# Running the masked weight's first products ahead of the layer norm, on raw x

## The chip, the cores and the metric

The kernel runs on one core of a Trainium2 chip (trn2). The time is the device time of one execution in microseconds (us), taken as the median of several runs. The core has a matrix engine (TensorE, "PE" in the profile; its weight loads are "PEld"), three engines for elementwise work (VectorE "DVE", ScalarE "ACT", GpSimd "POOL") and SyncE ("SP"), which issues the DMAs here. Each engine takes its instructions in the order in which the program lists them.

## The reference

```python
x  = data                                  # (2, 1024, 512), float32
xn = layernorm(x)                          # per token, eps 1e-5, no weight
w_masked = weight * (32x32 block of mask has a non-zero sum)    # (512, 512)
s  = einsum('bsk,nk->bsn', xn, w_masked)
nx = rmsnorm(xn) * ln_w
h  = silu(nx @ gate_w.T) * (nx @ up_w.T)   # 1792 features
g  = silu(h @ down_w.T)
out = x + s * g
```

All is float32. The 2048 tokens are four token tiles of 512 columns, and the 512 features are four chunks of 128 rows.

## The kernel before

All matrix products are done by a two-level Strassen-like scheme (the Winograd variant) on blocks. The outer level splits rows of the weight, features and tokens in two and has seven products per weight group, `q` = 1 to 7; each of them is again seven products of a 128x128 weight with a 128x512 operand, `m` = 1 to 7. One `(g, q)` is an *instance* of seven products (`instance`); a product is two matmul instructions in the profile.

There are eight weight groups. Groups 0 to 6 are pieces of the gate and up weights; group 7, called `G`, is the masked weight. The program runs `q` = 1 and 2 of all groups first (phase 1: 16 instances, group after group), then `q` = 6, 5, 7, 3, 4 of all groups (phase 2), then the product with the down weight (`down_instance`). For `q` = 1 and 2 only token tiles 0 and 1 are needed.

Nothing is scheduled by the compiler: each step is entered with `at(pos, fn)`, the events are sorted by `pos`, and each engine gets its instructions in that order. One position is the time of one product on TensorE. Instance `j` puts its products at `7*j` plus 0, 2, 3, 4, 6, 8 and 12 (for `m` = 1, 5, 2, 6, 3, 7, 4) unless the table `EARLY` says otherwise. `T(us)` turns a planned time at the start into a position.

The start: x tiles 0 and 1 are loaded by token rows, `stats` takes mean and variance on VectorE, `factors` makes scale and shift (ScalarE square root, VectorE reciprocal), `normalise` applies them, TensorE transposes the tiles (`transpose`), and `evacuate` copies them out of PSUM. TensorE meanwhile multiplies an identity (`warm`). Token tiles 2 and 3 are treated otherwise: they are loaded already transposed (`load_xt`), and their scale and shift, which then lie along the columns, are turned into rows on TensorE (`fac_rows`), stored to DRAM, read back as a broadcast over the partitions (`fac_bc`) and applied on GpSimd (`scale_xt`).

PSUM banks are taken by tag: X has 3, Y 2, Z 1 and V 2 (`PSB`). A V bank is used for anything short-lived: transposed tiles, `fac_rows`, mask sums, gates.

GpSimd also makes the sums of weight blocks (`inner_a`, four ops per instance pair, around seven positions ahead of it), some of the operand differences (`inner_b`, `outer_b`) and the masking (`mask_a`). Group `G` comes last in phase 1, so its mask is loaded at position 15, summed at 46 to 53 (`mask_rows`), gathered over 32x32 blocks by a small matmul (`mask_blocks`) at 79.5, and applied around position 90. The sums that group `g` keeps for phase 2 lie in `acc` (four tiles) and are stored to `acc_dram[g]`; the finished part of `s` goes to `s_dram`.

Of the kernel before, what the change touches and what calls it, by code (L numbers as in the profile page):

```python
# [14 lines left out]
P = 128  # L15
# [16 lines left out]
def tile_masked_linear_gated_ffn(  # L32
# [22 lines left out]
    fac_dram = tc.dram_tile([2, 2, W], F32, name="fac_dram")  # L55
# [11 lines left out]
    EARLY = {}  # L67
# [42 lines left out]
    def constants():  # L110
        nc.gpsimd.memset(eps2, EPS * EPS)
        make_identity(nc, ident)
        nc.scalar.activation(stat_0, eps2, AF.Sqrt)
        nc.gpsimd.memset(blockones, 0.0)
        for b in range(P // BLK):
            nc.gpsimd.memset(blockones[b * BLK : (b + 1) * BLK, b * BLK : (b + 1) * BLK], 1.0)
# [4 lines left out]
    fac = small.tile([P, 2, 2, TT], F32, tag="fac", name="fac", bufs=1)  # L121
    rms = small.tile([P, NTT, TT], F32, tag="rms", name="rms", bufs=1)

    def load_x(t):
        for i in range(TT):
            xt[t, i] = mem[:, first_slot[("B6", "vc", "v5", "B4")[t]] + i, :]
            nc.sync.dma_start(xt[t, i], x[(t * TT + i) * P : (t * TT + i + 1) * P, :])
# [6 lines left out]
    def factors(t, i=0, n=TT):  # L134


        if t < 2:
            scl = small.tile([P, n], F32, tag="scl", name=f"scl_{t}_{i}", bufs=3)
            nb = small.tile([P, n], F32, tag="nb", name=f"nb_{t}_{i}", bufs=3)
        else:  # L140
            scl, nb = fac[:, t - 2, 0, :], fac[:, t - 2, 1, :]
# [69 lines left out]
    def fac_rows(t):  # L211
        b = bank("V", f"fac_rows_{t}")
        nc.tensor.transpose(b[: 2 * TT, :P], fac[:, t - 2].rearrange("p f i -> p (f i)"), ident)
        rows = small.tile([2 * TT, P], F32, tag="rows", name=f"fac_sb_{t}")
        nc.scalar.copy(rows, b[: 2 * TT, :P])
        nc.sync.dma_start(fac_dram[t - 2].rearrange("f (i p) -> (f i) p", p=P), rows)
        for f in range(2):
            fac_bc[t, f] = mem[:, F["B6"] + 3 + 2 * (t - 2) + f, :]
            nc.sync.dma_start(fac_bc[t, f], fac_dram[t - 2, f].unsqueeze(0).to_broadcast([P, W]))
# [62 lines left out]
    def operand(q, m):  # L282
# [17 lines left out]

    def load_a(g, K):
        aq[g, 0, K] = mem[:, F["a1"] + 2 * (g % 3) + K, :]
        nc.sync.dma_start(aq[g, 0, K], gu[g, 0, K] if g < G else wm[0, K])
# [50 lines left out]
    def mask_blocks():  # L354
        pm = bank("V", "pm")
        nc.tensor.matmul(pm[:, :64], blockones, mask_sums.rearrange("p a b -> p (a b)"), start=True, stop=True)
        nc.vector.tensor_scalar(keep.rearrange("p a b -> p (a b)"), pm[:, :64], 0.0, None, ALU.is_gt)

    def mask_a(v, R, K):
        v = v.rearrange("p (b j) -> p b j", j=BLK)  # L360
        k = keep[:, 2 * R + K, :].unsqueeze(2).to_broadcast([P, 16, BLK])
        nc.gpsimd.tensor_tensor(v, v, k, ALU.mult)

    def inner_a(g, part, k0=0, n=2):

        if part == 1:
            i, si, qs = F["a1"] + 2 * (g % 3), F["s"] + 2 * (g % 2), (1, 2)
# [17 lines left out]
    def instance(j, g, q, prior, dest, after):  # L385
# [4 lines left out]
        seeded = j > 1  # L390

        def mm(m, tag, key, first):
            if first and key not in st:
                st[key] = bank("Y" if key == "z" and j == 1 else tag, f"{key}_{j}")
            nc.tensor.matmul(st[key], weights(g, q, m), operand(q, m), start=first and not (key == "z" and seeded),  # L395
                             stop=True, skip_group_check=True)

        def seed():
# [4 lines left out]
            else:  # L403
                st["s1"] = slot("s2" if j else "s5", f"s1_{j}")
# [23 lines left out]
        for off, m, tag, first, snapshot, out in (  # L428
# [8 lines left out]
            key, pos = tag.lower(), 7 * j + off  # L437
# [3 lines left out]
            elif out:  # L441

                pos += 2.3 if prior is None and m == 2 and seeded else 1
# [6 lines left out]
    def group(g, where):  # L450
# [3 lines left out]
        acc, v5, c1 = tiles(F["acc"] + 4 * (g % 2)), tiles(F["v5"] + 4 * (g % 2)), tiles(F["c1"] if g % 2 else F["vc"])  # L454
# [17 lines left out]
        def done(R, Hh, tiles):  # L472
# [3 lines left out]
            def after(i, pos):  # L476
                r, n = divmod(i, 2)
                if g == G:
                    at(pos + 1, lambda: nc.sync.dma_start(s_dram[2 * R + r, 2 * Hh + n], tiles(i)))
# [10 lines left out]
        def summed(dst, src, into, then=None, engines=(pool,) * 4):  # L490
# [9 lines left out]
            1: (None, acc, nothing),  # L500
            2: (acc, c1, done(0, 0, c1)),
# [16 lines left out]
        at(7 * where[g, 1] + 15, lambda: nc.sync.dma_start(acc_dram[g], sums))  # L518
# [117 lines left out]
    def down_instance(o, q, where_, prior, dest, after):  # L636
# [78 lines left out]
        if last_set:  # L715
            at(where_(17) + 0.1, base_of_last)
            for part, pos in zip(parts, (where_(23), where_(24), where_(25))):
# [6 lines left out]
    order = [(g, q) for g in range(G + 1) for q in (1, 2)]  # L724
# [4 lines left out]
    T = lambda us: (us - 14.0) / 0.86  # L729
    EARLY.update({(0, 1): T(10.4), (0, 2): T(11.3), (1, 1): T(12.1), (1, 2): T(13.0), (0, 0): T(11.5), (1, 0): 4.3,  # L730
                  (0, "z"): 2.2, (1, "z"): 4.5})
    SILU = 26.2
    at(T(-10), constants)
    at(T(-10), load_x, 0)
    at(T(-10), lambda: nc.scalar.dma_start(lnw_sb, ln_w))

    at(T(-10), lambda: nc.gpsimd.tensor_copy(mem[:, F["a1"], 0:1], xt[0, 0][:, 0:1]))
    at(T(-10), load_a, 0, 0)
    at(T(-10), load_x, 1)
    at(T(-10), load_a, 0, 1)  # L740

    at(T(9.95), lambda: nc.gpsimd.memset(mem[:, F["a1"] + 2, 0:1], 0.0))
    for K in range(2):
        at(T(9.96), load_a, 1, K)
    at(T(9.96), load_x, 2)
    for K in range(2):
        at(T(9.96), load_a, 2, K)
    at(T(9.96), load_x, 3)
# [8 lines left out]

    at(T(1.4), lambda: warm(22, bank("V", "idle")))
    plan(T(4.9), 0, factors(0, 0, 2))
    plan(T(7.1), 0, factors(0, 2, 2))  # L760
    for t, p, step in ((1, T(12.5), 0), (3, 23.2, 0.6), (2, 36.1, 1.2)):
        plan(p, step, factors(t))
    for us, i, h in ((5.9, 0, 0), (6.0, 0, 1), (6.1, 1, 0), (7.2, 1, 1), (7.95, 2, 0), (8.4, 2, 1), (7.95, 3, 0), (8.4, 3, 1)):
# [223 lines left out]
```

## Time and profile before

| | |
|---|---|
| median of 3 runs | 507.12 us (506.67 to 507.19) |
| profiled execution: span from the first to the last instruction | 504.8 us |
| PE / DVE / ACT / POOL busy | 99% / 74% / 37% / 71% of the span |
| matmul 128x512, mean of one | 593 ns (two to a product; they are pipelined) |
| POOL 128x512 tensor op | 1322 ns mean |
| DVE 128x512 tensor op | 686 ns mean |
| ACT 128x512 copy | 573 to 597 ns mean |
| DMA | 124.75 MB, 247 GB/s mean over the span |

The profile is of one execution, whose span is 504.8 us; the runs' times have a median 2.3 us above that. A line of a timeline gives the start, the duration, engine, source line, operation, the tiles written and read, the count, and in square brackets how long the engine had been idle before and what ended that. `L98` is the helper `add`, through which all tensor-tensor ops go. "Waits" and "idle" are inferred from semaphore events.

### The profile page before, as it was taken

What the parts mean: (1) busy time and instruction counts of PE and PEld (TensorE: products, weight loads), DVE (VectorE), ACT (ScalarE), POOL (GpSimd) and SP (SyncE); (2) the same over time, 40 slices, a digit from 0 to 9 for tenths busy, and PEclk for the clock granted to TensorE, in tenths of its full rate; (3) what the DMA queues carried; (4) which work ended last, traced back from release to release, by engine and by line L of the source; (5) the groups of instructions that cost most, each with busy time, mean ns of one, the idle gap of its engine ahead of it and who ended that gap; (6) DMA issues with size and microseconds to landing.
All of it is one profiled execution on the core that took longest, in us unless ns stands there. A gap on an engine that the chain in (4) does not pass through costs nothing.

```text
span 504.8 us, 4923 instructions
## 1 busy us (share of the span) xinstructions
PE 499.2 (99%) x1231; PEld 227.4 (45%) x1231; DVE 375.6 (74%) x578; ACT 188.1 (37%) x362; POOL 358.8 (71%) x301
## 2 busy tenths in 40 slices
PE   8999999999999999999999999999999999999996
PEld 7444444444444444444444444444444444444444
DVE  6887887876968969697896969879657644377636
ACT  6667775734535363443535333330101101001111
POOL 5629997464886959879696999985672764649960
PEclk9999999999999999999999999999999999999999
DMA  6878746368178594876949475599996798467362
GB/s 208 306 234 335 292 168 250 123 251 293 62 245 295 186 329 181 295 240 244 335 154 317 179 265 213 216 351 387 365 335 221 253 389 311 130 238 269 106 229 84
DMA packets 62221, 124.75 MB, mean 247 GB/s; under 512 B 5968, under 2 KB 13552, under 8 KB 60144
## 3 DMA queue, kind: packets, MB, share of 16 engines
q1 hardware_dynamic: 62048, 124.43, 69.1%
q8 instruction: 10, 0.16, 0.1%
q14 instruction: 19, 0.16, 0.1%
q10 hardware_dynamic: 144, 0.00, 0.0%
HBM read 78.25 MB, written 46.15 MB: 246 GB/s over the span
## 4 chain that ended last, share of the span: by engine, by line
PE 97%; DVE 1%; ACT 1%; DMA 1%; issue 0%; DVEq 0%; ACTq 0%
PE x L395 38%; PE y L395 19%; PE dx L643 15%; PE z L395 10%; PE dy L643 8%; PE dz L643 5%; PE dv L643 1%; PE pt L165 1%; DMA mem<-in_x 1%; DVE mem L98 0%; ACT mem L158 0%; DVE st L131 0%; DVE mem L633 0%; ACT silu L626 0%; ACT scl L150 0%
## 5 line engine op out<-in xcount | busy, mean ns | idle before, releaser
L98 POOL TENSOR_TENSOR mem<-mem 128x512 f32<-128x512 f32 (+4 forms) x261 | 322.1, 1257 | 111.6 <-ACT mem L423 30.5
L395 PE MATMUL x<-mem 128*128 128x512 f32 x448 | 211.7, 593 | 0.0
L395 PEld LDWEIGHTS x<-mem 128*128 128x128 f32 x448 | 84.6, 190 | 107.3 <-issue 89.7
L98 DVE TENSOR_TENSOR mem<-x,mem 128x512 f32<-128x512 f32 x137 | 93.4, 686 | 42.1 <-PE x L395 40.4
L395 PE MATMUL y<-mem 128*128 128x512 f32 x224 | 114.6, 593 | 0.1
L643 PE MATMUL dx<-mem 128*128 128x512 f32 x174 | 78.3, 592 | 0.0
L98 DVE TENSOR_TENSOR mem<-mem 128x1536 f32<-128x1536 f32 (+3 forms) x50 | 66.9, 1342 | 6.9 <-PE dx L643 4.4
L98 DVE TENSOR_TENSOR mem<-y,mem 128x512 f32<-128x512 f32 x96 | 65.9, 686 | 7.9 <-PE y L395 6.5
L402 ACT COPY z<-x 128x512 f32<-128x512 f32 x54 | 30.9, 573 | 94.7 <-PE x L395 91.7
L395 PEld LDWEIGHTS y<-mem 128*128 128x128 f32 x224 | 42.2, 190 | 53.1 <-issue 46.5
L395 PE MATMUL z<-mem 128*128 128x512 f32 x112 | 57.3, 593 | 0.0
L643 PEld LDWEIGHTS dx<-mem 128*128 128x128 f32 x174 | 33.1, 190 | 41.6 <-issue 40.9
L643 PE MATMUL dy<-mem 128*128 128x512 f32 x98 | 44.5, 592 | 0.0
L461 ACT ACTIVATE gate<-mem 128x512 f32<-128x512 f32 x56 | 32.7, 602 | 20.4 <-DVE mem L98 15.9
L466 DVE TENSOR_TENSOR mem<-gate,mem 128x512 f32<-128x512 f32 x56 | 38.1, 682 | 1.9 <-ACT gate L461 1.5
L616 POOL TENSOR_TENSOR mem<-mem 128x512 f32<-128x512 f32 x16 | 25.8, 1619 | 13.6 <-DMA mem<-s_dram 13.4
L626 ACT ACTIVATE silu<-mem 128x512 f32<-128x512 f32 x15 | 9.0, 602 | 64.6 <-DVE mem L98 48.3
L395 PEld LDWEIGHTS z<-mem 128*128 128x128 f32 x112 | 21.1, 190 | 25.9 <-issue 21.4
L98 DVE TENSOR_TENSOR mem<-z,mem 128x512 f32<-128x512 f32 x41 | 28.1, 685 | 2.8 <-PE z L395 2.7
L643 PEld LDWEIGHTS dy<-mem 128*128 128x128 f32 x98 | 18.6, 190 | 23.4 <-issue 23.2
L98 DVE TENSOR_TENSOR mem<-dx,mem 128x512 f32<-128x512 f32 x16 | 11.1, 691 | 20.3 <-PE dx L643 20.2
L643 PE MATMUL dz<-mem 128*128 128x512 f32 x56 | 25.2, 592 | 0.0
(86 smaller groups left out, 286.9 us busy)
## 6 DMA issues: line engine op xcount, KB each, us to landing
h_dram<-mem SPq DMA_DIRECT2D x98, 256.0 KB, 2.2
mem<-h_dram SPq DMA_DIRECT2D x28, 768.0 KB, 6.7
mem<-in_gu SPq DMA_DIRECT2D x42, 256.0 KB, 3.9
acc_dram<-mem SPq DMA_DIRECT2D x8, 1024.0 KB, 4.0
mem<-acc_dram SPq DMA_DIRECT2D x8, 1024.0 KB, 6.1
mem<-in_x_t SPq DMA_DIRECT2D x24, 256.0 KB, 5.5
mem<-in_x SPq DMA_DIRECT2D x16, 256.0 KB, 4.5
s_dram<-mem SPq DMA_DIRECT2D x16, 256.0 KB, 6.1
```

The costliest lines, as they stand in the source:

```text
L98: eng.tensor_tensor(o, a, b, op)
L165: nc.tensor.transpose(pt[t, c][:, i * P : (i + 1) * P], xt[t, i][:, c * P : (c + 1) * P], ident)
L395: nc.tensor.matmul(st[key], weights(g, q, m), operand(q, m), start=first and not (key == "z" and seeded), stop=True, skip_group_check=True)
L402: nc.scalar.copy(st["z"], st["x"])
L461: nc.scalar.activation(gate[key], t(), AF.Silu)
L466: nc.vector.tensor_mul(a(), gate[key], b())
L616: at_later.append(lambda: nc.gpsimd.tensor_tensor(s_tile, s_tile, rms_bc[t], ALU.mult))
L626: nc.scalar.activation(b[0][:, part], y[:, part] if source is None else source(), AF.Silu)
L643: nc.tensor.matmul(st[key], w(), b(), start=first and key != "z", stop=True, skip_group_check=True)
```

## The change

Group `G` now comes first in phase 1 (`order`), as instances 0 and 1. Its operands are token tiles 0 and 1 of x itself, loaded transposed and not normalised (`load_raw`, `raw_b`). Since the layer norm of a token is `scl * x + nb`, its product with a weight row is `scl` times the raw product plus `nb` times the sum of that row. The row sums are taken on TensorE with a column of ones (`row_sum`, `row_sums`), and the eight finished tiles (four kept sums, four of `s`) are multiplied by the broadcast `scl` on GpSimd, the outer product of `nb` and the row sums is made on ScalarE, and GpSimd adds it (`amend`, steps 0, 1, 2). For this, tiles 0 and 1 get broadcast factors through `fac_rows` as tiles 2 and 3 have.

Group 0 and all that goes with it move 14 positions later (`S`); the plan's times at the start have a new origin (`R_`); the work between positions 62 and 104 is moved by less and less (`late`), and phase 2 stays where it was. The mask's first two quarters are loaded first of all; the loads of the start are issued in one row without the two small ops that held some of them back. The warm-up is 9 and 2 products instead of 22.

```diff
+        nc.gpsimd.memset(ones, 1.0)
-    fac = small.tile([P, 2, 2, TT], F32, tag="fac", name="fac", bufs=1)
+    fac = small.tile([P, NTT, 2, TT], F32, tag="fac", name="fac", bufs=1)
...
     def fac_rows(t):
         b = bank("V", f"fac_rows_{t}")
-        nc.tensor.transpose(b[: 2 * TT, :P], fac[:, t - 2].rearrange("p f i -> p (f i)"), ident)
+        nc.tensor.transpose(b[: 2 * TT, :P], fac[:, t].rearrange("p f i -> p (f i)"), ident)
...
+    def load_raw(c, t):
+        xr[c, t] = mem[:, F["B7" if c > 1 else "B5"] + 2 * t + c % 2, :]
+        nc.sync.dma_start(xr[c, t], x_t[c, t])
+
+    def raw_b(q, m, eng):
+        b11, b12, b21, b22 = (xr[2 * (q - 1) + k, n] for k in (0, 1) for n in (0, 1))
+        o = mem[:, F["B3"] + 2 + q if m == 4 else F[("B5", "B7")[q - 1]] + m - 1, :]
+        a, b = {5: lambda: (b12, b11), 6: lambda: (b22, rop[q, 5]), 7: lambda: (b22, b12),
+                4: lambda: (b21, rop[q, 6])}[m]()
+        add(eng, o, a, b, ALU.subtract)
+        rop[q, m] = o
...
+    def row_sum(K, r, k):
+        if not rs:
+            rs[0] = bank("V", "rsums")
+        c = 2 * K + r
+        nc.tensor.matmul(rs[0][:, c : c + 1], aq[G, 0, K][:, (2 * k + r) * P :][:, :P], ones, start=k == 0, stop=k == 1,
+                         skip_group_check=True)
+
+    def row_sums():
+        nc.scalar.copy(rsum[:, 0:2], rs[0][:, 0:2])
+        nc.vector.tensor_add(rsum[:, 2:4], rs[0][:, 2:4], rsum[:, 0:2])
+
+    def amend(i, src, o, part, of, step):
+        r, n = divmod(i, 2)
+        if step == 0:
+            add(pool, o, src, fac_bc[n, 0], ALU.mult)
+        elif step == 1:
+            nc.scalar.mul(part, fac_bc[n, 1], rsum[:, of + r : of + r + 1])
+        else:
+            add(pool, o, o, part)
...
+            kept, s11 = F["B5"], F["B7"]
+            for n, i in enumerate((0, 1, 3, 2)):
+                for step, pos in enumerate((AMEND[0], AMEND[1] - 1.5, AMEND[1])):
+                    at(pos + 1.5 * n, lambda i=i, n=n, step=step: amend(i, acc1(i), mem[:, kept + i, :],
+                                                                        mem[:, kept + 4 + n % 3, :], 0, step))
+                    at(pos + 6 + 1.5 * n, lambda i=i, n=n, step=step: amend(i, c1(i), mem[:, s11 + i, :],
+                                                                            mem[:, s11 + 4 + n % 3, :], 2, step))
+                at(AMEND[1] + 7 + 1.5 * n, lambda i=i: nc.sync.dma_start(s_dram[i // 2, i % 2], mem[:, s11 + i, :]))
+            at(AMEND[1] + 6, lambda: nc.sync.dma_start(acc_dram[G], slots(kept, 4)))
...
-    order = [(g, q) for g in range(G + 1) for q in (1, 2)]
+    order = [(g, q) for g in (G, *range(G)) for q in (1, 2)]
...
+    R_ = lambda us: (us - 8.7) / 0.86
+    S = 14
+    late = lambda p: p + S if p < 62 else p + S * (104 - p) / 42 if p < 104 else p
+    RAW.update({jm: R_(5.05 + 0.86 * k) for k, jm in enumerate(
+        ((0, 1), (0, 2), (0, 5), (0, 6), (0, 3), (0, 7), (1, 1), (0, 4), (1, 2), (1, 5), (1, 6), (1, 3), (1, 7)))})
+    RAW[1, 4] = R_(17.0)
+    AMEND = (22.0, 34.0)
...
-    at(T(1.4), lambda: warm(22, bank("V", "idle")))
+    at(R_(1.4), lambda: warm(9, bank("V", "idle")))
+    at(R_(4.4), lambda: warm(2, bank("V", "idle2")))
+    for K, p in ((0, 3.5), (1, 7.65)):
+        at(R_(p), mask_rows, 0, K)
+        at(R_((4.2, 8.45)[K]), mask_blocks, K, 1)
+        at(R_((4.5, 8.9)[K]), mask_keep)
+    for us, b0, b1, eng in ((4.55, 0, 4, dve), (4.6, 8, 12, dve), (4.65, 4, 8, pool), (4.7, 12, 16, pool)):
+        at(R_(us), lambda b0=b0, b1=b1, eng=eng: mask_a(aq[G, 0, 0], 0, 0, eng, b0, b1))
+    at(R_(8.95), lambda: mask_a(aq[G, 0, 1], 0, 1, dve))
+    for us, q, m, eng in ((6.0, 1, 5, dve), (6.6, 1, 6, dve), (7.3, 1, 7, pool), (8.6, 1, 4, pool),
+                          (12.0, 2, 5, dve), (13.2, 2, 6, dve), (13.3, 2, 7, pool), (14.5, 2, 4, pool)):
+        at(R_(us), raw_b, q, m, eng)
...
-    for t, p, step in ((1, T(12.5), 0), (3, 23.2, 0.6), (2, 36.1, 1.2)):
+    for t, p, step in ((1, R_(19.2), 0), (3, S + 23.2, 0.6), (2, S + 36.1, 1.2)):
         plan(p, step, factors(t))
...
+    at(S + 5.5, fac_rows, 0)
+    at(S + 5.9, fac_rows, 1)
...
-    at(25.2, fac_rows, 3)
+    at(S + 25.2, fac_rows, 3)
```

## The prediction

> **What bounds it now.** I read the page's span, busy lines and chain that ended last, then timelines: the first 22 us, GpSimd's, and all engines and SyncE around 31 to 36 us.
>
> ```profile
> span 504.8 us, 4923 instructions
> PE 97%; DVE 1%; ACT 1%; DMA 1%; issue 0%; DVEq 0%; ACTq 0%
> ```
>
> TensorE (PE) is the chain from 8.8 us on. The end moves only if PE starts useful work earlier, does more, or stops. The start, from the timeline (start, duration, engine, line, op):
>
> ```profile
> 1.37 6.97 PE L756 MATMUL idle<-ident 128*128 128x128 f32 x44 [1.37 <-POOL ident masks.py:199]
> 3.50 0.69 DVE L131 BATCH_NORM_STATS2 st<-mem 128x6 f32<-128x512 f32 x1 [3.50 <-DMA mem<-in_x]
> 13.11 1.38 DVE L156 TENSOR_SCALAR mem<-mem,scl,nb 128x256 f32<-128x256 f32 x4
> 15.69 1.13 PE L395 MATMUL y<-mem 128*128 128x512 f32 x2
> 17.11 0.14 PEld L165 LDWEIGHTS pt<-ident,mem 128*128 128x128 f32 x1 [0.26 <-ACT mem L173]
> 19.69 0.68 DVE L98 TENSOR_TENSOR mem<-pt,mem 128x512 f32<-128x512 f32 x1
> ```
>
> Until 8.2 us PE only warms up. VectorE (DVE) normalises x from 3.50 to 14.49. From 15.69 (group 0's product m=5, position 2) PE is dense: a product (two matmuls) each 0.86 us. So the prize is a few us. At 17.11 PE waits for a PSUM bank of tag V until ScalarE (ACT) has read it: there are two V banks.
>
> GpSimd's timeline:
>
> ```profile
> 20.45 4.26 POOL L98 TENSOR_TENSOR mem<-mem 128x512 f32<-128x512 f32 x5 [0.69 <-DVE mem L98]
> 29.94 3.02 POOL L98 TENSOR_TENSOR mem<-mem 128x256 f32<-128x256 f32 x4 [5.23 <-ACT mem L316]
> 39.10 15.08 POOL L98 TENSOR_TENSOR mem<-mem 128x512 f32<-128x512 f32 x14 [6.13 <-DMA mem<-fac_dram]
> ```
>
> The first row is `inner_b` (2,4), 1.24 us, and `inner_a` of group 1 (four of about 0.7); the second is `inner_a` of group 2; then it waits for the broadcast factors and is full. The factors' route, from the timelines of all engines and of SyncE (SP):
>
> ```profile
> 31.27 0.30 ACT L150 ACTIVATE fac<-agg,eps 128x4 f32<-128x4 f32 x1
> ...
> 33.74 0.27 PE L213 MATMUL fac_rows<-ident,fac 128*8 128x128 f32 x1
> ...
> 34.33 0.34 SPq L216 DMA_DIRECT2D fac_dram<-fac_sb  x1
> 35.69 0.90 SPq L219 DMA_DIRECT2D mem<-fac_dram  x2
> ```
>
> ACT's copy of the rows starts at 34.05 (0.25); the broadcast is issued 1.36 after the store, and GpSimd has it at 39.10, 3.4 after that. PE takes the `fac_rows` transposition in its order, between products.
>
> **Part 1, the start.** The raw group's 14 products (12.04 us) move in front, and group 0 is moved by as much: the change gains if PE's dense point goes from 15.69 to less than 27.73. DVE decides. Up to its last normalise it has 9.6 us of work now (8 statistics at 0.82 from start to start, 3 pairs of small factor ops at 0.37, 6 half normalises at 0.32) in 11.0 us, so 1.4 of waits. Added ahead of that point, with 0.60 from start to start for a 128x512 op (19.69, 20.29, 20.89 in DVE's rows): nine evacuations of raw sums, 5.4; four `raw_b`, 2.4; two `mask_rows` at 0.66 and two `mask_keep` at 0.2, 1.7; `mask_a`, one whole and two quarters, 1.0; `row_sums` 0.2. That is 10.8, in all 20.4: from 3.50 to 23.9 without a wait. Waits, from laying the queues out in their order: 1.5 for the first `pm` (18 warm-up matmuls at the 0.21 us that one takes before 5.0 us hold PE to about 5.3, and `mask_blocks` is behind them), 0.6 for the second, 0.5 for product (0,2), 0.5 for the last square root, 0.6 in bits: 27.6. The last transpositions and group 0's m=5 follow 1.6 later (ACT's halves end last): 29.2 against 27.73, **1.5 us lost**. With only today's 1.4 of waits it is 0.8 gained; with waits half as long again, 3.4 lost. `row_sum` costs PE 8 x 0.21 (what the `pm` pair took between its neighbours), inside this DVE-bound stretch.
>
> **Part 2, the factor rows of tiles 0 and 1.** They need a V bank at S+5.5. One bank holds `pt_1_2` until S+10.05; the other, `pt_1_3`, is read last by `inner_b` (2,6), the 19.69 row, which now ends 13.5 later, at 33.87. PE is there at 31.4 and stands 2.5 us, and 0.6 more for the second `fac_rows`, which wants the bank after ACT's copy. Rows at 34.45, store 34.5, broadcast 35.85, landed 39.2. Tile 1's store is on SP behind tile 0's broadcasts: landed 41.3.
>
> **Part 3, amend.** 16 GpSimd ops at 1.235 (the 39.10 row's first: 39.10, 40.34, 41.57) are 19.8 us. Its free time between 21.7 and 39.10, less the eight `inner_a` ops, is 11.8. Its queue after: `inner_b` (2,4) ends at 35.2, two `inner_a` at 36.6; waits for factors to 39.2; multiply to 40.4, `inner_a` to 41.1, waits to 41.3, multiply and `inner_a` to 43.25, six multiplies to 50.65, first add to 51.9. Now the wait that this makes: step 1 for the fourth tile (ACT, position 37.0) writes the buffer that this add reads (`n % 3`), so ACT stands from about 45 to 51.9. Behind it on ACT is the square root of `factors(3)` (S+23.2 = 37.2), behind that DVE's reciprocal (and what DVE has queued), behind that PE's `fac_rows` of tile 3 (39.2). So 51.95 + 0.48 for ACT's multiply + 0.30 + 0.4 = **53.2** on PE. Its row is 33.74 now, and 45.78 with 14 products before it: **7.4 us late**. PE waits once for the longest chain, so the 7.4 holds the start's 1.5 and the bank's 3.1, and 2.8 remain for this stop.
>
> What is late next: ACT's seed of instance 6 comes at 58.1 against a use at 57.6; `inner_a` (3) at 67.8 against 68.9; `inner_a` (5) at 92.0 against 93.0. `acc_dram[G]` and four `s_dram` stores hold SP until the adds (58 to 63) with `h_dram` stores and `load_a(4)` behind; their uses are past 64. All are covered by that stall to within 0.5 us; uncovered they cost 1 to 2, which I keep for the range. The other moves (`late`, the mask loads, `inner_a(G)` off GpSimd at position 91) lie beside a dense PE and are taken at nothing.
>
> Sum: 504.8 + 7.4 = 512.2 of span; the median of the runs is 2.3 above the span, so **514.5**. If the factors were there at once, the first add would end at 36.6 + 1.4 + 9 x 1.235 = 49.1: 4.6 late; with a start 2.3 better as well, 2.3. If each store took SP the 3.4 us that it took at 47.32 instead of 1.36: 11.4 late.
>
> One rule bears on the stall. The windows of the warm-up show the matmuls (first x) per us rise from 7 to 10 at 5.0 us, 3.6 us after PE began, with the granted clock at 1.00 in both:
>
> ```profile
> 4.00:5.00 1.00, 1.00 (x7) 1.00 (x6) 1.00 1.00 373
> 5.00:6.00 1.00, 1.00 (x10) 1.00 (x10) 1.00 0.87 184
> ```
>
> So idle before the program is paid with 3.6 us at half rate; no row shows it after a pause in the program. By the row alone a pause costs 0 to 1.8. The Trainium skill ("TensorE: Matmul & The Clock Gate", section "Why this matters for your kernels") wants no PE gap above some 3 us between bursts, since one idle window halves the clock; my gaps are 3.1 and 2.8 us, about at it, and by the rule one merged gap would make the estimate 516.3.
>
> **Rivals.** (a) Only the start counts: amend is hidden, since ACT and GpSimd have more slack than I see. For it: ACT is 37% busy, GpSimd 71%. Against: both wait in order, and the 39.10 row is full from its start. 507.12 + 1.5 + 0.2 for two transpositions = 508.8. (b) Faster: DVE's waits shrink to nothing (20.4 us of work, then 1.6: dense at 25.5, 2.2 gained) and amend is hidden too: 505.1 with the 0.2. It decides where DVE waits under 2.2 us in the start. For it: 8 us of PE warm-up are to be had. Against: the first `pm` alone costs 1.5. (c) The change does not do what it says: group 0 is dense at 27.7, just 12.04 later, so nothing came forward, and all else is covered: 507.1, the same.
>
> **Numbers.** The chain through amend 0.70 (likeliest value 514.5; own range 509.4 to 518.5), (a) 0.14, (b) 0.11, (c) 0.05. A measurement of this kernel can tell about 0.2%, 1.0 us. Faster 0.11, same 0.06, slower 0.83 (the chain, and nearly all of (a)). Low end 506.4, between (b) and (c), high end 518.5 (11.4 late).
>
> **What would show it.** PE's first raw product at 6.2, group 0's m=5 near 29; PE idle before `fac_rows` near 31 with DVE as releaser, and again before 53 with ACT or DVE; ACT idle some 6 us with GpSimd as releaser; GpSimd without a gap from 41 to 100. A dense PE from 30 us on, or a first amend add before 46, proves me wrong.

## The result, and the profile after

The changed kernel takes 524.32 us (median), the kernel before 507.01 us beside it: the ratio is 1.0338 (95% interval 1.0321 to 1.0354). The forecast was 514.5 us, its range ended at 518.5. The direction was right, the size was not. One of the four times of the changed kernel (537.1 us) and three of four of a run below (`no_wait`, 530.2 to 531.2 us) lie more than 10 us above the others, at a lower mean granted clock; why is not known, and no figure here uses them.

From the page of the changed kernel (span, busy times, shares of the chain that ended last):

```profile
span 522.8 us, 5005 instructions
...
PE 506.5 (97%) x1231; PEld 228.6 (44%) x1231; DVE 387.8 (74%) x594; ACT 190.5 (36%) x367; POOL 383.5 (73%) x324
...
PE 76%; DVE 3%; ACT 1%; DMA 1%; issue 1%; SPq 0%; DVEq 0%; ACTq 0%
```

The chain was 97% PE before. The timeline of the changed kernel on PE (in the brackets: idle before, and what ended it) shows the places that the forecast named:

```profile
18.41 1.10 PE L440 MATMUL x<-mem 128*128 128x512 f32 x2 [1.78 <-DVE mem L98]
19.48 1.81 PE L440 MATMUL y<-mem 128*128 128x512 f32 x2
...
31.03 1.10 PE L440 MATMUL y<-mem 128*128 128x512 f32 x2
...
35.67 0.27 PE L211 MATMUL fac_rows<-ident,fac 128*8 128x128 f32 x1 [2.25 <-DVE mem L98]
...
57.66 0.38 PE L211 MATMUL fac_rows<-ident,fac 128*8 128x128 f32 x1 [3.95 <-DVE fac L146]
57.83 1.92 PE L440 MATMUL x<-mem 128*128 128x512 f32 x2
```

The first line is a pause in the start that the forecast did not have; 31.03 is group 0's m=5 (forecast 29.2); 35.67 is the bank wait; 57.66 is `fac_rows` of tile 3 (forecast 53.2). The lines at 19.48 and 57.83 are products at half rate, 1.8 to 1.9 us instead of 1.0 to 1.1. The same kernel's GpSimd, ScalarE and SyncE:

```profile
35.70 2.74 POOL L98 TENSOR_TENSOR mem<-mem 128x512 f32<-128x512 f32 x3 [0.69 <-DVE mem L98]
40.78 1.96 POOL L98 TENSOR_TENSOR mem<-mem 128x512 f32<-128x512 f32 x2 [2.34 <-DMA mem<-fac_dram]
45.14 17.08 POOL L98 TENSOR_TENSOR mem<-mem 128x512 f32<-128x512 f32 x16 [2.40 <-DMA mem<-fac_dram]
...
55.72 0.72 ACT L312 ACTIVATE mem<-mem,rsum 128x512 f32<-128x512 f32 x1 [4.18 <-POOL mem L98]
56.35 0.28 ACT L148 ACTIVATE fac<-agg,eps 128x4 f32<-128x4 f32 x1
...
36.26 0.35 SPq L214 DMA_DIRECT2D fac_dram<-fac_sb  x1
37.51 0.82 SPq L217 DMA_DIRECT2D mem<-fac_dram  x2
38.42 0.28 SPq L214 DMA_DIRECT2D fac_dram<-fac_sb  x1
40.97 0.80 SPq L217 DMA_DIRECT2D mem<-fac_dram  x2
```

GpSimd waits for tile 0's factors to 40.78 and for tile 1's to 45.14, and is then full to 106.8 with one gap of 1.4 us. ScalarE stands 4.18 us for the buffer of the fourth part, and the square root of tile 3 comes behind it: the chain of the forecast, step for step, only later.

**Where the time went.** In the two profiled executions the time of each product (a pair of matmuls) in the changed kernel is set against that of the same product before, less 0.8585 us for each product that was put in front of it. What is left is its lag. It is 17.8 us at the last product, and it grows at a few places only:

| place (time after) | growth of lag, us | forecast |
|---|---|---|
| start, to group 0's m=5 (31.0) | 3.3 | 1.5 |
| bank wait and second `fac_rows` (33.3 to 36.4) | 3.1 | 3.1 |
| products at half rate (36.8 to 40.2) | 1.4 | 0 to 1.8 |
| wait before `fac_rows` of tile 3 (53.5 to 57.7) | 4.2 | 2.8 |
| products at half rate (57.3 to 60.7) | 1.4 | in the 1.8 |
| small waits (78 to 110) | 2.7 | covered |
| VectorE chain of phase 2 (148, and 153) | 1.5 | 0 |

The half-rate products of the start (19.8 to 23.2) are not a place of their own: the run without amend, below, has none of them in its profile, and its m=5 comes at 30.98 all the same.

### The profile page after: what moved, and what is told of

Same layout as the page of the kernel before. It is cut to its first block, busy times and chain, and to the rows that moved or that the text cites. A ratio compares the mean times of both kernels' runs of the same rounds, so it can differ in the third digit from the quotient of the medians.

```text
span 522.8 us, 5005 instructions
## 1 busy us (share of the span) xinstructions
PE 506.5 (97%) x1231; PEld 228.6 (44%) x1231; DVE 387.8 (74%) x594; ACT 190.5 (36%) x367; POOL 383.5 (73%) x324
## 4 chain that ended last, share of the span: by engine, by line
PE 76%; DVE 3%; ACT 1%; DMA 1%; issue 1%; SPq 0%; DVEq 0%; ACTq 0%
PE x L440 28%; PE dx L703 14%; PE y L440 14%; PE dy L703 8%; PE z L440 7%; PE dz L703 5%; DVE mem L98 3%; PE dv L703 1%; DMA mem<-acc_dram 1%; ACT held L250 0%; ACT mem L355 0%; ACT gate L508 0%; DVE mem L693 0%; ACT silu L686 0%; DVE mem L513 0%
## 5 line engine op out<-in xcount | busy, mean ns | idle before, releaser
L98 POOL TENSOR_TENSOR mem<-mem 128x512 f32<-128x512 f32 (+4 forms) x285 | 348.6, 1249 | 105.7 <-ACT mem L468 27.7
L440 PE MATMUL x<-mem 128*128 128x512 f32 x448 | 216.6, 601 | 3.5 <-DVE mem L98 3.2
L98 DVE TENSOR_TENSOR mem<-x,mem 128x512 f32<-128x512 f32 x141 | 95.8, 685 | 38.4 <-PE x L440 36.8
L440 PE MATMUL y<-mem 128*128 128x512 f32 x224 | 116.9, 604 | 0.0
L98 DVE TENSOR_TENSOR mem<-mem 128x1536 f32<-128x1536 f32 (+3 forms) x54 | 72.5, 1347 | 7.3 <-PE dx L703 4.4
L98 DVE TENSOR_TENSOR mem<-y,mem 128x512 f32<-128x512 f32 x96 | 65.8, 686 | 10.8 <-PE y L440 8.8
L447 ACT COPY z<-x 128x512 f32<-128x512 f32 x48 | 27.5, 574 | 84.6 <-PE x L440 77.6
L98 DVE TENSOR_TENSOR mem<-z,mem 128x512 f32<-128x512 f32 x43 | 29.4, 683 | 3.5 <-PE z L440 2.8
L703 PEld LDWEIGHTS dy<-mem 128*128 128x128 f32 x98 | 18.6, 190 | 23.4 <-issue 23.2
```

Of the source, the lines that this page charges most:

```text
L98: eng.tensor_tensor(o, a, b, op)
L440: nc.tensor.matmul(st[key], weights(g, q, m), operand(g, q, m), start=first and not (key == "z" and seeded), stop=True, skip_group_check=True)
L447: nc.scalar.copy(st["z"], st["x"])
L703: nc.tensor.matmul(st[key], w(), b(), start=first and key != "z", stop=True, skip_group_check=True)
```

## The experiments

Two theories. **Load**: the 16 GpSimd ops (19.8 us) do not fit into what GpSimd had free; the backlog costs its time through whichever wait is left. **The chain**, the rival: the time is lost at the named stops, the bank and ScalarE's part buffer (the one that the fourth tile's product is written to), so that taking a stop away gives its time back. A third, **arrival**, came up with the first results: not the work but the late broadcasts cost, for everything behind the first amend op stands for them.

### 1. Taking away one stop, the other, both, and the whole amend

```diff
late_rows
-    AMEND = (22.0, 34.0)
+    AMEND = (25.0, 34.0)
-    at(S + 5.5, fac_rows, 0)
-    at(S + 5.9, fac_rows, 1)
+    at(S + 10.3, fac_rows, 0)
+    at(S + 10.6, fac_rows, 1)
part4 (a buffer of its own for the fourth part; the same for s11 with free + 2)
-    mem[:, kept + 4 + n % 3, :]
+    mem[:, kept + 4 + n if n < 3 else F["free"] + 1, :]
both: the two edits together
no_amend: no fac_rows 0 and 1, no amend(); s_dram and acc_dram[G] stored from the raw sums
```

> The factor rows of tiles 0 and 1 are taken at S+10.3 and S+10.6, when the V bank of pt_1_2 is free, and the multiplies begin at position 25. Chain theory: PE's pause at 33 to 36.4 and the half-rate window after it go (4.5 us), but the factors come no earlier, ScalarE is held as long, and the pause before the rows of tile 3 (57.7 us) grows by what is saved: 522 to 525. Sum theory (each pause counts by itself): 519.8.

> The fourth tile's product nb x row sum gets a buffer of its own, so ScalarE no longer waits for GpSimd's add. Chain theory: the 4.2 us pause before the rows of tile 3 and its half-rate window (1.4) go: about 518.7, up to 520.5 if GpSimd's backlog shows at inner_a of group 2 or 3. Load theory (16 more ops on GpSimd set the end whoever waits): 523 to 524.5.

> Both edits. Chain theory: both pauses and both windows go, 524.3 - 4.5 - 5.6 = 514.2, up to 517 where GpSimd's backlog of some 8 us now shows at inner_a of group 3. Load theory: 521 or more.

> Leaves out the scaling and shifting of the raw group's eight tiles and the factor rows of tiles 0 and 1; the raw sums are stored as they are. What is left is the start. If all the rest comes from amend and its waits: 507.0 + 3.3 = 510.3 (1.6 of it a half-rate window). If the 4 us lost between 78 and 148 us come from the moved work and not from amend: 514.

| run | us | ratio (95%) |
|---|---|---|
| late_rows | 523.80 | 1.0331 (1.0313 to 1.0348) |
| part4 | 523.72 | 1.0333 (1.0318 to 1.0348) |
| both | 523.20 | 1.0328 (1.0311 to 1.0344) |
| no_amend | 512.68 | 1.0120 (1.0105 to 1.0136) |

The stops went and the time stayed. Without the bank wait, TensorE still stood 3.5 us before `fac_rows` of tile 3 (4.0 in the changed kernel), and now also 1.2 us at 49 and 1.3 at 65 us. Without ScalarE's stop, it stood 2.6 us at 68 to 71; without both, 1.1 us at 47 and 2.6 at 67 to 70 us. The waits of the run without both stops, from 62 to 72 us (engine and line, what it waited for, us in total, times, longest):

```profile
DVE mem L98 <- DMA h_dram<-mem: 4.1, 1, 4.1
...
PE x L440 <- DVE mem L98: 2.6, 1, 2.6
```

VectorE stood for an `h_dram` store, which stood on SyncE behind `acc_dram[G]` and the first `s_dram` store, which waited for GpSimd's last additions. GpSimd there:

```profile
40.23 1.28 POOL L98 TENSOR_TENSOR mem<-mem 128x512 f32<-128x512 f32 x1 [1.40 <-DMA mem<-fac_dram]
44.63 36.98 POOL L98 TENSOR_TENSOR mem<-mem 128x512 f32<-128x512 f32 x34 [3.12 <-DMA mem<-fac_dram]
```

So the chain as the place of the loss falls. The amend as a whole costs 11.6 us (524.3 less 512.7), through any of three routes. Of the 5.7 us that are left without it (512.7 less 507.0), lag says that 3.3 are the start and 2.5 lie at 84 to 92 and at 136 to 142 us. That these come from the work moved by `late` and by the new order is argued from where they lie; no run tests it.

### 2. Work or waits

Five kernels change the work and the waits apart. `half3` leaves the four kept tiles raw (8 GpSimd ops). `narrow` lets all 16 ops cover 128 of 512 columns (0.45 us each). `no_wait` replaces the factors by rows of x that are loaded early, so its masked product is not scaled by the layer norm's factors; it does without the two `fac_rows` as well. The first two also without the wait: `half_nw`, `narrow_nw`. All begin the multiplies at position 25 and have the factor rows, where they are kept, at S+10.3, as late_rows has; the edits are against late_rows.

```diff
half3
-    at(pos + 1.5 * n, ... amend(i, acc1(i), mem[:, kept + i, :], ...))
-    at(AMEND[1] + 6, lambda: nc.sync.dma_start(acc_dram[G], slots(kept, 4)))
+    at(22, lambda: nc.sync.dma_start(acc_dram[G], first_sums))
narrow (the same in step 2)
-    add(pool, o, src, fac_bc[n, 0], ALU.mult)
+    add(pool, o[:, :P], src[:, :P], fac_bc[n, 0][:, :P], ALU.mult)
no_wait
-    at(S + 10.3, fac_rows, 0)
-    at(S + 10.6, fac_rows, 1)
+    at(S - 6, stand_in)      # fac_bc[t, f] <- x[t : t + 1, :].to_broadcast([P, W])
```

> As the second run with half of the amend (the four kept tiles left raw, factor rows at S+10.3), but the raw kept sums are stored at position 22 instead of 25, as in the run without amend, so that the store has landed before ScalarE and VectorE write their buffers again (in the second run they stood 4.3 and 3.4 us for it, and TensorE lost 2.8 at 50 us). By the sum (half the ops, all of the wait: 5 us short): 515 to 517. If the store is not what held them: 518.8 again.

> All of the amend stays (factor rows at S+10.3, broadcasts, ScalarE's parts, stores, every wait and the order of every queue), but its 16 GpSimd ops cover 128 of their 512 columns, so they should take some 0.35 to 0.45 us each instead of 1.235, about 6 us in all. Left out: the other 384 columns. Load theory: 512.7 to 515 us, as without any amend. Arrival theory (GpSimd stands for the two broadcasts, some 7 us): 518 or more. Both by their sum: 6 + 7 - 11.8 = 1 us short: 513 to 516.

> All 16 GpSimd ops and ScalarE's parts stay, but the factors of tiles 0 and 1 are replaced by rows of x that are loaded as broadcasts at position 8, so they are there long before the first multiplication; the factor rows of tiles 0 and 1 (two transpositions, two copies, two stores, four broadcasts) are left out. The values of the masked product are therefore not scaled by the layer norm's factors. Load theory: 19.8 us still do not fit into 11.8, so 518 to 521, with a wait of TensorE before the factor rows of tile 3 or at the operands of groups 2 and 3. Arrival theory: 513 to 515, as without amend. If both count by their sum (19.8 - 11.8 = 8 us short instead of 15): 515 to 519.

> The same kernel as the run with stand-in factors (full amend work, no wait for broadcasts), since only one of its four times, 519.7 us, agreed with its profile and three were 530. Work alone (19.8 us of GpSimd against 11.6 that it has free): 519 to 520. If the 530 is its own: three of four at 530 again.

> Both at once: the stand-in factors (rows of x loaded as broadcasts at position 8, no factor rows of tiles 0 and 1) and half of the amend (the four kept tiles left raw, their sums stored at position 22). 9.9 us of GpSimd work against 11.6 free, and no wait. By the account of work and waits, as without any amend: 512.5 to 514. If half of the work costs half of the 7 us that the whole work costs without waits: 516.

> Both at once: the stand-in factors and amend ops on GpSimd that cover 128 of their 512 columns (0.45 us each, 7.2 us in all), with ScalarE's parts, stores and every queue's order kept. By the account, as without any amend: 512.5 to 514; then the 6.5 us that the narrow ops cost beside the late broadcasts are the price of those waits alone. If the number of ops, ScalarE's parts or the stores cost by themselves: 516 or more.

| us (over 512.7) | with the late broadcasts | factors there at once |
|---|---|---|
| 16 ops, all columns | 523.8 (11.1), late_rows | 519.6 (6.9), no_wait_again |
| 16 ops, 128 columns | 519.2 (6.5), narrow | 515.3 (2.6), narrow_nw |
| 8 ops, all columns | 517.0 (4.3), half3 | 514.1 (1.4), half_nw |
| none | | 512.7, no_amend |

The intervals of the ratios are narrow against these steps: 1.0227 to 1.0258 for narrow, 1.0190 to 1.0220 for half3, 1.0241 to 1.0272 for no_wait_again, 1.0155 to 1.0189 for narrow_nw, 1.0127 to 1.0158 for half_nw. Of the first run of `no_wait` only the time of 519.7 is used; its repetition gave 519.2 to 520.7 in all four.

Read down a column: narrowing the ops saves 4.6 us with the waits and 4.3 without. Read across: having the factors at once saves 4.2 us with full ops, 3.9 with narrow ones and 2.9 with half of them. So both theories are right in part, and the parts nearly add: **4.2 us for having the factors late, 4.3 for the 12.6 us of GpSimd's work that narrowing takes out, and 2.6 that stay even with narrow ops and no wait**, 11.1 in all. Two things are inside these parts. Of the 4.2, some 0.75 is not lateness but the two `fac_rows` and the wait of 0.47 between them (by lag, in late_rows, narrow and half3 alike). Of the 4.3, some 1.7 is a half-rate window: behind the start, the profiles of late_rows and no_wait_again have one each (at 56.3 and 61.3 us), those of the other five none. Leaving out half of the amend, ScalarE's parts and buffers with it, brings the price to 1.4 of 6.9 without waits: below the amount of work that fits, it is nearly free. By lag the 2.6 of narrow_nw lie at 54 us (1.0) and 71 to 78 us (1.7). Its GpSimd waits for ScalarE's parts:

```profile
53.80 0.46 POOL L98 TENSOR_TENSOR mem<-mem 128x128 f32<-128x128 f32 x1 [2.64 <-ACT mem L318]
54.94 7.97 POOL L98 TENSOR_TENSOR mem<-mem 128x128 f32<-128x128 f32 x8 [0.68 <-ACT mem L318]
```

That these waits make up the 2.6 is argued, not shown: no run took out ScalarE's parts alone.

What was free can be read in the run without amend:

```profile
35.64 4.27 POOL L98 TENSOR_TENSOR mem<-mem 128x512 f32<-128x512 f32 x5 [0.69 <-DVE mem L98]
45.13 3.01 POOL L98 TENSOR_TENSOR mem<-mem 128x256 f32<-128x256 f32 x4 [5.22 <-ACT mem L355]
54.51 15.06 POOL L98 TENSOR_TENSOR mem<-mem 128x512 f32<-128x512 f32 x14 [6.37 <-DMA mem<-fac_dram]
```

From 39.9 to 54.5, where the work on tile 3 starts, GpSimd has 14.6 us, of which 3.0 are taken: 11.6. The 19.8 of the amend are 8.2 over, near the 6.9 measured without waits. The 9.9 of half of it fit, and 1.4 was measured. The 7.2 of the narrow ops fit too, and 2.6 was measured: the rule of the excess is not the whole account.

### 3. Two runs with half of the amend that had a fault of their own

```diff
half_amend: as half3, but fac_rows as in the changed kernel, and the store of the raw sums
+    at(AMEND[1] + 6, lambda: nc.sync.dma_start(acc_dram[G], first_sums))
half2: as half3, with the store
+    at(AMEND[0], lambda: nc.sync.dma_start(acc_dram[G], first_sums))      # 25
```

> The four kept tiles are left raw: their eight GpSimd ops, four ScalarE parts are left out, the four tiles of s are amended as in the changed kernel, with the same factor rows, broadcasts and first position on GpSimd of the rest. Load theory (GpSimd's 16 ops of 1.235 us do not fit into the 11.8 us that it had free, so half of them, 9.9 us, do): 513 to 516 us, the waits before the factor rows of tile 3 and at 70 us gone or under 1 us each, the bank wait of about 3 us at 33 us still there with its half-rate window. Arrival theory (what counts is that the broadcasts land at 40.7 and 45.1 us, and that everything behind the first amend op on GpSimd waits for them, however few ops there are): 519 us or more.

> As the run with half of the amend, with two differences: the raw kept sums are stored at position 25, before the next group writes their buffers (in the first such run the store stood on SyncE until 56.6 us and landed at 63.8, and held ScalarE for 7.4 us), and the factor rows of tiles 0 and 1 are at S+10.3, past the V bank's reader. Left out: the amend of the four kept tiles. Load theory (8 GpSimd ops, 9.9 us, fit into the 11.8 us that GpSimd had free): 513 to 515 us, as without any amend. Arrival theory (GpSimd stands for the broadcasts some 7 us in all, and that alone makes what is behind it late): 518 or more. If both count, by their sum (9.9 + 7 - 11.8 = 5.1 us short): 515 to 518.

527.1 us and 518.8 us: half the work, and in the first case slower than the whole. The raw sums' buffers are written again by the next groups, and their store, issued on SyncE at 56.6 us in the first, landed at 63.8; ScalarE waited 7.4 us for it and TensorE 8.4. In the second, ScalarE and VectorE waited 4.3 and 3.4. With the store at 22 they waited no more, and it was 517.0. An experiment that leaves work out can make another buffer the bottleneck; neither run is used for the price of the amend.

### 4. The additions on VectorE

```diff
stt (with late_rows)
-        elif step == 1:
-            nc.scalar.mul(part, fac_bc[n, 1], rsum[:, of + r : of + r + 1])
-        else:
-            add(pool, o, o, part)
+        elif step == 2:
+            nc.vector.scalar_tensor_tensor(o, fac_bc[n, 1], rsum[:, of + r : of + r + 1], o, ALU.mult, ALU.add)
```

> The whole amend is done, but its second part (ScalarE's product and GpSimd's add) becomes one VectorE op for each tile, which reads the broadcast shift, multiplies by the row sum and adds; GpSimd keeps the eight multiplications, 9.9 us; ScalarE has no part of it and no buffer to wait for. The factor rows of tiles 0 and 1 are at S+10.3, past the V bank's reader. Load theory: 513 to 516 us, with eight VectorE ops of about 0.7 us more. If VectorE's queue is the next to stand (its new ops wait for GpSimd's multiplications, ahead of operands that TensorE needs): 517 to 520, with TensorE waiting for VectorE. Arrival theory: 519 or more, with TensorE waiting for GpSimd.

522.02 us, ratio 1.0289 (1.0265 to 1.0313): 1.8 us better than late_rows. That is above what the load theory and VectorE's queue gave; it lies in the open range of arrival, but TensorE waited for VectorE and not for GpSimd. GpSimd's ops were halved, but the wait before `fac_rows` of tile 3 was still there (3.3 us at 53.2, VectorE the releaser), and a second one of 1.9 us at 63. VectorE's timeline says why (three of the eight new rows):

```profile
45.41 0.74 DVE L312 SCALAR_TENSOR_TENSOR mem<-mem,rsum 128x512 f32<-128x512 f32 x1
...
48.73 1.55 DVE L312 SCALAR_TENSOR_TENSOR mem<-mem,rsum 128x512 f32<-128x512 f32 x1
...
50.80 1.15 DVE L312 SCALAR_TENSOR_TENSOR mem<-mem,rsum 128x512 f32<-128x512 f32 x1
```

The first came just ahead of GpSimd's next op and took 0.74, and that op, at 45.49, took 1.78 instead of 1.27; one more, at 59.12, did the same. The other six, beside GpSimd ops, took 1.15 to 1.59. Three of the eight stand ahead of tile 3's reciprocal, and VectorE became the engine that is late.

### 5. The start

All four are built on the run without amend, where group 0's m=5 is at 30.98.

```diff
start_order
-    (12.0, 2, 5, dve), (13.2, 2, 6, dve)
+    (10.9, 2, 5, dve), (12.4, 2, 6, dve)
no_mask: mask_rows, mask_blocks, mask_keep of quarters 0 and 1 moved to late(46.1) to late(79.45); no mask_a on aq[G, 0, K]
no_sums: inner_a(G, 1) left out, products 3, 5, 6, 7 of group G read plain blocks
tail: raw_b(2, 5) and raw_b(2, 6) left out, rop[2, 5] = b12, rop[2, 6] = b22
```

> The amend ops and the factor rows of tiles 0 and 1 are left out, as in the run without amend, and the two raw_b operands of product 5 and 6 of the second raw instance come first on VectorE (10.9 and 12.4 instead of 12.0 and 13.2), ahead of the statistics between them, so that TensorE should not stand 1.9 us at 16.5 us. If the start is bound by the sum of VectorE's work: 512.7 us again (within 0.5), the pause only moves to a later product. If the pause itself is what is lost: about 510.8 us, group 0's first late product at 29.1 instead of 31.0. Either way the granted clock tells whether a half-rate window after 19.7 us goes with the pause.

> As the run without amend, and the mask work of the start is taken out: the two quarters' sums are made later, beside those of the other two (so that phase 2 has them), and group G's first weight is not masked at all in phase 1. VectorE has 2.7 us less to do ahead of its last normalisation, and TensorE's first raw product needs no mask. If the start is VectorE's sum of work: group 0's first late product at 28.0 to 28.6 us instead of 31.0, time 509.7 to 510.3. If it is bound by the loads or by TensorE's own 14 products and transpositions: 512 or more.

> As the run without amend, and GpSimd's eight small sums of group G's weight blocks (128x128 each, 7 to 16 us) are left out: the raw products 3, 5, 6 and 7 then read plain blocks. VectorE's own work stays. In the changed kernel VectorE's ops with two SBUF operands are longer beside GpSimd's (a pair 1.55 instead of 1.28 us, a small one of 0.16 took 0.86, the masking 1.07 instead of 0.69), some 1.3 us in all before 17 us. If that contention is in the bound of the start: group 0's first late product 0.8 to 1.5 us earlier than 31.0, time 511.2 to 512. If VectorE's waits elsewhere take it up: 512.7 again.

> As the run without amend, and two of VectorE's four raw operand differences (products 5 and 6 of the second raw instance; 0.60 us each from start to start, at 14.5 and 17.6 us) are left out, the products read a plain raw tile. Taking out 2.7 us of mask work before 13 us brought group 0's first late product forward by only 0.7 us. If VectorE's dense run from 13 us to its last normalisation is the bound of the start: that product at 29.8 instead of 31.0, time 511.5. If TensorE's pause at 16.5 to 18.4 us (which waits for these two) is in it as well: 29 and 510.8. If neither: 512.7.

| run | us | ratio (95%) | group 0's m=5 at |
|---|---|---|---|
| no_amend | 512.68 | 1.0120 (1.0105 to 1.0136) | 30.98 |
| start_order | 513.45 | 1.0131 (1.0116 to 1.0146) | 31.70 |
| no_mask | 512.81 | 1.0121 (1.0106 to 1.0136) | 30.35 |
| no_sums | 512.18 | 1.0107 (1.0090 to 1.0123) | 31.16 |
| tail | 512.13 | 1.0115 (1.0095 to 1.0136) | 29.11 |

The scatter must be known first: in the profiles of the fourteen kernels whose start is that of the changed kernel, this product begins between 29.92 (both) and 31.84 us (late_rows), with 30.9 in the middle. Three of the four runs lie inside; only tail, 1.8 us below the middle, lies outside. Taking 2.7 us of VectorE's work out ahead of 13 us thus gave 0.6 in its profile, less than the scatter, where 2.4 to 3 were expected; taking 1.2 out behind 13 us gave 1.8. The times of the runs do not settle it: two of tail's four are 511.3 (the profiled one among them), the other two 513.0 and 513.5, no better than no_amend. As far as one profile of each shows, then, it is not VectorE's whole sum that binds, as the forecast had it. Up to about 13 us the loads of raw x and the first products set the pace (without the mask, VectorE's first op waits to 7.08 for raw x), and from then to its last normalisation VectorE is dense and is the bound. The surplus of tail's gain over 1.2 may go with TensorE's pauses around 16.5 to 19 us (1.8 in the changed kernel, 0.3 and 1.05 in no_amend), which are gone there; that is argued only. Reordering alone moved that pause to 18.1 to 20.2 and gained nothing. GpSimd's small sums made no difference that stands out of the scatter.

### 6. How long a pause halves the clock

The kernel before, with seven pauses made of chains of ScalarE copies between two small matmuls:

```diff
+    for i, k in enumerate((1, 3, 5, 7, 9, 12, 16)):
+        at(150.5 + 35 * i, pause, k)
```

> The kernel before with seven artificial pauses of TensorE at about 131, 161, 191, 221, 251, 281 and 311 us: a small matmul, then a chain of 2, 4, 6, 8, 10, 13 and 17 small ScalarE copies, then a small matmul that reads the chain's end; everything else as before. Pauses of about 0.7 to 4 us. If only an idle stretch of more than about 3 us halves the granted clock, one or two of the seven are followed by a half-rate window, and the time is that before plus the pauses (about 15 us) plus 2 to 4. If 2 us are enough, as the start of the changed kernel suggests, three to five are, and it is 5 to 9 more than the pauses. If a window is judged as a whole on a fixed grid, a pause of 2 to 3 us counts only where it falls well inside one window of 3.4 us.

528.95 us, in one run. The pauses were 0.47, 0.92, 1.36, 1.81, 2.26, 2.93 and 3.82 us long (13.6 in all). Windows of this kernel around the last three pauses (stretch, its length, PE busy (x matmuls), then PEld, DVE, ACT, POOL, the granted clock, DMA share, GB/s):

```profile
268.30:271.70 3.40, 1.14 (x6) 0.58 (x4) 1.91 (x4) 1.99 (x11) 3.32 (x4) 1.00 0.80 308
271.70:275.10 3.40, 3.40 (x6) 1.85 (x7) 0.69 (x1) 0.40 (x1) 3.26 (x3) 0.50 0.73 280
302.40:305.80 3.40, 1.59 (x6) 0.76 (x4) 2.40 (x4) 1.55 (x10) 3.32 (x4) 1.00 0.70 269
305.80:309.30 3.50, 2.39 (x7) 1.28 (x8) 0.83 (x2) 1.44 (x6) 3.42 (x4) 1.00 0.70 268
...
340.00:343.40 3.40, 1.82 (x4) 1.26 (x5) 0.00 (x0) 1.84 (x8) 3.32 (x3) 0.50 0.69 264
```

The pause of 2.26 us is followed by a clock of 0.50, that of 2.93 is not, because it fell across the border of two windows (1.86 and 1.07 us in them). The pause of 3.82 (from 337.76) put two windows at 0.50. So the rule of a fixed grid holds, and a rule that goes by the length of the pause alone does not: see the end. Pauses and three windows of 1.7 us explain 18.7 us of the 22.2 by which the time is above the kernel before (506.8); the remaining 3.5 were not looked into.

## Why the prediction failed

**Point by point.** Part 2, the bank wait, held: 3.1 us forecast and measured, and late_rows, which takes it away, shows it is worth nothing by itself. Part 3's chain is in the trace link by link (ScalarE's stop, square root, reciprocal, `fac_rows`), at 57.66 instead of 53.2. Part 1's direction held (1.5 forecast, 3.3 lost). Its waits were right and its work too small: up to its last normalisation (3.49 to 29.32 us) VectorE was idle 3.8 us, where 3.7 were added up, and busy 22.0, where 20.4 were. Two figures of the working do not come out of its own rows, and neither matters: the added ops make 10.7 us, not 10.8, and GpSimd's free time is 11.4 (the idle of 5.23 and 6.13 in its rows), not 11.8. The 2.3 us between span and time compares different executions; within one it is 1.7 to 1.8.

**The step that failed** is the sentence "All are covered by that stall to within 0.5 us; uncovered they cost 1 to 2", with the moved work "taken at nothing" behind it. The amend was priced at the first places where it touches TensorE, the bank wait and the stop (3.1 and 2.8, so 5.9 us), and all readers behind were taken as covered by that stop. The runs gave 11.6 for it. In the changed kernel's lag, 11.9 us were lost at `fac_rows` of tile 3 (7.4 forecast) and 17.8 at the end (still 7.4 forecast): 5.9 us behind the stop had been priced at nothing. They are 1.4 of half rate, 2.7 of small waits, 1.5 of phase 2 and 0.3 in bits.

The stop does not pay off GpSimd's debt: while TensorE stands, the GpSimd queue still has its 8 us too much and its waits ahead of it, and what it feeds comes late again. late_rows, part4 and both show it: with either stop or both gone, the same time is lost elsewhere. Worked out afterwards, a sum from the prediction's own figures would have been nearer: 19.8 against 11.8 free is 8.0 over, some 4 for waiting, so some 12. That this meets 11.6 so well is partly luck, since half-rate windows and ScalarE's parts, which are not in it, were in the measured time.

**Terms that were mis-sized.** The stop itself came 4.5 us later than forecast (57.66 against 53.2). The second broadcast landed at about 45.1, not 41.3, which alone moved the first addition's end from 51.9 to 55.7. Of these 3.8 us, 1.8 are the start (the first `fac_rows` at 35.67, not 33.87); the others are SyncE, which held its own store 2.55 us before issuing the broadcast at 40.97 (1.36 in the kernel before), and the landing, which took 4.1 us (3.4 before).

The half-rate windows were left out of the sum and are 1.4 us each, twice. The prediction had named them: by its own row a pause costs 0 to 1.8, and the Trainium skill ("TensorE: Matmul & The Clock Gate", section "Why this matters for your kernels") asks for no gap above some 3 us. The loss of clock and its size were right, but in these runs shorter ones do it too: 2.25 and 0.35 us at 33.4 to 36.3, inside one window, were enough.

"Taken at nothing" for the moved work was wrong by 2.5 us in the run without amend; the same two places show in the changed kernel. 1.2 of these go with one VectorE op in phase 2, which reads two SBUF tiles: in the changed kernel's timelines it starts while GpSimd is at work and lasts until 0.54 after GpSimd's op ends (146.68). TensorE waits for the VectorE op right behind it:

```profile
145.57 1.65 DVE L98 TENSOR_TENSOR mem<-mem 128x512 f32<-128x512 f32 x1
...
145.14 1.54 POOL L98 TENSOR_TENSOR mem<-mem 128x640 f32<-128x640 f32 x1
```

In the kernel before, the op of the same line and shape comes one place earlier in VectorE's order, takes 0.68 (128.91), and it is GpSimd's op that is longer, 1.92.

**The rivals.** (a), only the start counts, and (b), faster, both needed the amend hidden: no_amend against the changed kernel says 11.6 us. Rival (b) also needed VectorE's waits in the start to be under 2.2 us; they were 3.8, and no_amend, with nothing but the new start and order, is slower by 5.7. (c) fails with the start's lag of 3.3. The range was too low because each unknown was bounded at one stop, and the bounds were not added.

## What to carry to other kernels

When an engine is given more work than it has free up to a deadline, price the whole excess, plus the time it stands for its inputs, against the end; a stop of the bounding engine does not hide what comes after it, unless the overloaded queue gets idle time out of it. Before moving a wait away, ask what else the late engine feeds: if there are three readers, removing one or two of them buys nothing. For work that needs a late operand (here the broadcast factors), halving the work saved 6.8 us here and having the operand early 4.2, and only both together made it nearly free (1.4 of 11.1 left).

## What the runs showed of the hardware

**The clock's window.** The granted clock in all these traces changes only on a grid of 3.413 us that runs through the execution (in the changed kernel at 19.75, 23.16, 36.82, 40.23, 57.30 and 60.71 us). Setting TensorE's idle time inside each grid window against the clock of the next one, over the twenty profiles: the 54 windows at full rate with 0.8 to 1.55 us idle are all followed by a full clock; of the thirteen with 1.75 to 1.93 us, ten by half rate; the ten with 2.2 us or more, all by half rate. So about half a window of idle is enough, and a pause of 1.78 us, as at 16.6 to 18.4 in the changed kernel, halved the next 3.4 us, while 2.93 us split over two windows did not. The windows of the changed kernel:

```profile
16.00:19.00 3.00, 1.22 (x6) 0.69 (x5) 2.97 (x7) 2.07 (x4) 0.91 (x2) 1.00 1.05 386
20.00:23.00 3.00, 3.00 (x6) 1.33 (x5) 2.71 (x7) 1.10 (x3) 3.00 (x4) 0.50 1.06 387
```

The page named above asks for no gap above some 3 us; these runs put the limit between 1.55 and 2.2 us inside one window.

**VectorE beside GpSimd.** In these traces VectorE ops with two SBUF operands are held by a GpSimd op in progress: 0.74 us where they came first and 1.15 to 1.59 where GpSimd did in stt, 0.68 and 1.65 in phase 2. The Trainium skill ("SBUF — State Buffer", section "SBUF: two separate sides") says that such ops and GpSimd's share a port that one of them holds for a whole instruction; the rows agree. In stt this made VectorE a poor place to unload GpSimd to: 1.8 us were gained of 11.
